# Window attention and vertical convolution on one core: pixels stored by pair of tiles, value products of both column parities at once, whole-tile products in parts

## The chip, the cores and the metric

The kernel runs on one core of a Trainium2 chip. The metric is the device time of one execution in microseconds; before the change it is 3428.8 us, the median of three runs (3424.14 to 3431.46). One more execution was recorded by the hardware profiler; its span is 3428.1 us, and all readings of the profile below are of that execution. The engines are called PE (matrix products; PEld is its weight load), DVE (vector), ACT (scalar), POOL (general) and SP (which issues the transfers here).

## The reference

Everything is float32. The input x is [2, 128, 256, 256]: two images of 128 channels. Two layers follow one another, each as "x = x + layer(groupnorm(x))", with 32 groups of 4 channels.

Layer 0 is a halo attention. A 1x1 projection gives q, k and v (4 heads of 32). Queries come in 8x8 windows, keys and values in 12x12 windows around them. The scores get a relative position term by row and by column, and a fixed mask:

```
table[0::2, :] = -np.inf
table[:, 0::2] = -np.inf
...
attn = jnp.einsum('bnd,bmd->bnm', q, k)
attn = attn + rel_pos_emb(q, rel_height, rel_width) + FIXED_MASK
attn = jax.nn.softmax(attn, axis=-1)
out = jnp.einsum('bnm,bmd->bnd', attn, v)
```

Because of the mask, a query sees only keys of its own row parity and its own column parity. So each window falls apart into four small attentions: for one row parity r and column parity c there are 4x4 = 16 queries and 6x6 = 36 keys. An output projection of 128x128 ends the layer.

Layer 1 is a 5-tap vertical convolution over all channels, a 3-tap depthwise one after it, times a grouped 3-tap horizontal product that is spread over channels.

## The kernel before, in words

**Units.** `attention_fast` walks over strips of 8 image rows (k = 0 to 63, 32 per image), and within each over the two row parities r. A pair (k, r) is a unit, u = 2k + r; there are 128. A strip has 32 windows side by side; two neighbours make a pair, so there are NPAIR = 16 pairs.

**Pixels.** `normalise(k)` turns ten rows of input into `f_xn`, a tile [128 channels, row parity, column parity, 131 columns, 6 rows]: for one parity, one column after the other, six rows each. There are two such tiles, used in turn. DVE does this with two scalings (L282), one per column parity; POOL copies the two rows that the strip shares with the one before (L275). A pair of windows needs 10 columns of one parity, 60 elements; it takes 64 from offset 48 n, and the next pair's begin two columns before these end. Thus the shared columns are stored once, and a pair's 64 elements of one column parity lie together, but those of the other parity lie far away.

**The products of a unit, in PE's order.** The order on every engine is written out by hand (`manual_schedule`).
- `biases` (L399, tile `f_s`): 32 matmul records of 32x64 that add the position terms.
- `scores` (L415, `f_s`): 128 records, 64 rows by 64 columns. ACT then takes the exponent (L424).
- `values` (L380, `f_pv`): the pixels are the stationary side, 64 of them, and the 128x128 value weights stream. One product for each of 16 pairs and 2 column parities, written to partitions 0 to 63 or 64 to 127. ACT copies one half of each bank to `f_vt`, DVE the other (L386).
- `coefficients` (L356, `f_pa`) for the next strip: 16 products of 64 columns with `f_xq`, pixels ordered by place, which POOL copies out of `f_xn` (`by_place`, L293, four copies per unit). ACT and DVE evacuate to `f_cf`.
- `attend` (L440, `f_o`): 128 records of 128 rows by 32 columns.
- `queries` (L333, `f_pq`), `keys` (L312, `f_pk`) of the next unit and `project` (L473, `f_py`) of this one: two products each, full 128x128 weights, 512 columns streamed, each filling one of the four rotating banks `ps_pj`.

A float32 product is one matmul in the program and two weight loads and two matmuls in the trace: 27,431 against 54,862. The products at the start of the kernel (L210) that fold the position tables into the query weights are cut in four per head.

`convolutions_fast` (L561 on) is the second layer. The change doesn't touch it.

Of the kernel before, what the change touches and what calls it, by code (L numbers as in the profile page):

```python
# [9 lines left out]
F32 = mybir.dt.float32  # L10
I32 = mybir.dt.int32
AF = mybir.ActivationFunctionType
ALU = mybir.AluOpType
# [6 lines left out]
P = 128  # L20
W = 256
HEADS = 4
DH = 32
NREL = 23
# [119 lines left out]
def attention_fast(tc, io, x1_d, norm, st_x, st_y, tags, ends):  # L144
# [6 lines left out]
    with ExitStack() as l0:  # L151
# [16 lines left out]
        wkT = wqkvT[:, P : 2 * P]  # L168
        wvT = wqkvT[:, 2 * P : 3 * P]

        xn = [cst.tile([P, 2, 2, XC, 6], F32, tag=f"f_xn{i}", name=f"f_xn{i}") for i in range(2)]
        kt = [
            [cst.tile([P, 2, XC, 6], F32, tag=f"f_kt{r}{i}", name=f"f_kt{r}{i}") for i in range(2)]
            for r in range(2)
# [6 lines left out]
            for g in range(2)  # L181
        ]

        xq = cst.tile([P, 4, 2, 4, 4, NPAIR], F32, tag="f_xq", name="f_xq")
        wb = cst.tile([P, 4, 4, HEADS, 16], F32, tag="f_wb", name="f_wb")
        for i in range(2):
            nc.gpsimd.memset(xn[i], 0.0)
# [7 lines left out]
        with ExitStack() as setup:  # L195
            sp = setup.enter_context(tc.tile_pool(name="f_setup", bufs=6))


            wq_nat = sp.tile([P, P], F32, tag="wq_nat", name="f_wq_nat", bufs=1)
            nc.sync.dma_start(wq_nat, io["w_q"])  # L200
            relT = sp.tile([P, 2 * NREL], F32, tag="relT", name="f_relT", bufs=1)
            nc.sync.dma_start(relT, io["relT"])
            g_rel = sp.tile([P, HEADS, 2 * NREL], F32, tag="g_rel", name="f_g_rel", bufs=1)
            for h in range(HEADS):
                pg = ps_pj.tile([P, 512], F32, tag="pj", name=f"f_pg_{h}")


                for o in (0, NREL):
                    for m in (0, 64):
                        nc.tensor.matmul(  # L210
                            pg[m : m + 64, o : o + NREL], wq_nat[32 * h : 32 * h + 32, m : m + 64],
                            relT[32 * h : 32 * h + 32, o : o + NREL], start=True, stop=True,
                        )
                nc.scalar.mul(g_rel[:, h, :], pg[:, : 2 * NREL], SCALE)
            for t in range(4):
                o = 11 - 2 * t
                for t1 in range(4):
                    nc.scalar.copy(wb[:, t, t1, :, 0:6], g_rel[:, :, o : o + 11 : 2])
                o = NREL + 11 - 2 * t
                for t2 in range(4):  # L220
                    nc.scalar.copy(wb[:, t2, t, :, 6:12], g_rel[:, :, o : o + 11 : 2])
            for s in range(NS):
                t = sp.tile([P, 8, W], F32, tag="sx", name=f"f_sx_0_{s}")
                nc.sync.dma_start(t, x[0, :, 8 * s : 8 * s + 8, :])
                norm.chunk(st_x[0], 4 * s, t)
# [27 lines left out]
        def load_rows(k):  # L253
# [4 lines left out]
            nc.sync.dma_start(t[:, 0:n, :], x[b, :, 8 * s : 8 * s + n, :])  # L258
            raws[k] = t

        def normalise(k):
            b, s = divmod(k, NS)
            if s == 0:
                norms[b] = norm.group(st_x[b], ps_pj, f"x{b}")
                st_y[b] = norm.new(f"st_y{b}", tags[(2 * b + 2) % 3])
                if b + 1 < NB:
                    st_x[b + 1] = norm.new(f"st_x{b + 1}", tags[(2 * b + 1) % 3])
            mean, rstd = norms[b]
            cur, prev = xn[k % 2], xn[(k + 1) % 2]
            cells = cur.rearrange("p r c j i -> p (r c) j i")  # L270
            if s == 0:
                nc.gpsimd.memset(cells[:, :, :, 0:1], 0.0)
                lo = 0
            else:
                nc.gpsimd.tensor_copy(  # L275
                    cells[:, :, :, 0:2], prev.rearrange("p r c j i -> p (r c) j i")[:, :, :, 4:6]
                )
                lo = 1
            hi = min(10, H - 8 * s) // 2
            rows = raws[k].rearrange("p (i r) (j c) -> p c r j i", r=2, c=2)  # L280
            for c in range(2):
                nc.vector.tensor_scalar(  # L282
                    cur[:, :, c, 1:129, 1 + lo : 1 + hi], rows[:, c, :, :, lo:hi], mean, rstd,
                    ALU.subtract, ALU.mult,
                )
            if hi < 5:
                nc.gpsimd.memset(cells[:, :, :, 1 + hi : 6], 0.0)

        def by_place(k, columns):
            cells = xn[k % 2].rearrange("p r c j i -> p (r c) j i")[:, :, 1:129, 1:5]  # L290
            for t2 in columns:
                for half in range(2):
                    nc.gpsimd.tensor_copy(  # L293
                        xq[:, t2, half],
                        cells[:, :, 64 * half : 64 * half + 64].rearrange(
                            "p a (m b) i -> p b i a m", b=4
                        )[:, t2],
                    )

        def old_keys(u):  # L300
            k, r = divmod(u, 2)
            if k % NS > 0:
                nc.gpsimd.tensor_copy(kt[r][k % 2][:, :, :, 0:2], kt[r][(k + 1) % 2][:, :, :, 4:6])

        def keys(u):
            k, r = divmod(u, 2)
            s = k % NS
            cur, xt = kt[r][k % 2], xn[k % 2]

            def part(c):  # L310
                pk = ps_pj.tile([P, 512], F32, tag="pj", name=f"f_pk_{u}_{c}")
                nc.tensor.matmul(pk, wkT, xt[:, r, c, 1:129, 2:6], start=True, stop=True)  # L312
                nc.scalar.copy(cur[:, c, 1:129, 2:6], pk.rearrange("p (j i) -> p j i", i=4))

            def top():

                pk = ps_pj.tile([P, 512], F32, tag="pj", name=f"f_pk_{u}_top")
                nc.tensor.matmul(pk, wkT, xt[:, r, :, 1:129, 0:2], start=True, stop=True)
                nc.scalar.copy(
                    cur[:, :, 1:129, 0:2], pk.rearrange("p (c j i) -> p c j i", c=2, i=2)  # L320
                )

            return ([top] if s == 0 else []) + [lambda c=c: part(c) for c in range(2)]

        def queries(u):

            k, r = divmod(u, 2)
            q = wk.tile([P, 2, NPAIR, 2, 32], F32, tag="q", name=f"f_q_{u}")
            qs[u] = q

            def part(c):
                pq = ps_pj.tile([P, 512], F32, tag="pj", name=f"f_pq_{u}_{c}")
                nc.tensor.matmul(  # L333
                    pq, wq_s, xn[k % 2][:, r, c, 1:129, 1:5], start=True, stop=True
                )
                for i in range(2):
                    nc.scalar.activation(  # L337
                        q[:, c, :, i], pq.rearrange("p (n x) -> p n x", n=NPAIR), AF.Copy,
                        scale=head[:, i : i + 1],
                    )  # L340

            return [lambda c=c: part(c) for c in range(2)]

        def coefficients(k, r):
# [3 lines left out]


            if r == 0:  # L350
                cfs[k] = wk.tile([P, 2, 4, 8, 2, 16], F32, tag="cf", name=f"f_cf_{k}")
            pa = ps_pj.tile([P, 512], F32, tag="pj", name=f"f_pa_{k}_{r}")
            for t in range(8):
                t2, t1 = 2 * r + t // 4, t % 4
                for half in range(2):
                    nc.tensor.matmul(  # L356
                        pa[64 * half : 64 * half + 64, 64 * t : 64 * t + 64],
                        wb[:, t2, t1].rearrange("p h x -> p (h x)"),
                        xq[:, t2, half, t1].rearrange("p a m -> p (a m)"), start=True, stop=True,
                    )  # L360
            src = pa.rearrange("p (t m e) -> p e m t", t=8, e=2)
            for i in range(2):
                dst = cfs[k][:, :, :, :, i, 8 * r : 8 * r + 8].rearrange("p e a n t -> p e (a n) t")
                if i == 0:
                    nc.scalar.activation(
                        dst, src, AF.Identity, bias=keep[:, 1:2], scale=keep[:, 0:1]
# [5 lines left out]

        def values(u, j):
            k, r = divmod(u, 2)
            xt = xn[k % 2].rearrange("p r c j i -> p r c (j i)")
            pv = ps_pj.tile([P, 512], F32, tag="pj", name=f"f_pv_{u}_{j}")
            for n in range(4):
                o = 48 * (4 * j + n)
                for c in range(2):
                    nc.tensor.matmul(  # L380
                        pv[64 * c : 64 * c + 64, P * n : P * n + P], xt[:, r, c, o : o + 64], wvT,
                        start=True, stop=True,
                    )
            for c in range(2):
                rows = slice(64 * c, 64 * c + 64)
                (nc.vector.tensor_copy if c else nc.scalar.copy)(  # L386
# [4 lines left out]
        def biases(u):  # L391

            k, r = divmod(u, 2)
            for e in range(2):
                for half in range(2):
                    for g in range(2):
                        rows = slice(64 * half + 32 * g, 64 * half + 32 * g + 32)
                        for c in range(2):
# [2 lines left out]
                                    "p n i x -> p (n i) x"  # L401
                                ),
                                hot[rows, e],
                                cfs[k][rows, e, 2 * r + c].rearrange("p n i x -> p (n i x)"),
                                start=e == 0, stop=False, skip_group_check=True,
                            )

# [59 lines left out]
        def project(u):  # L467
# [2 lines left out]
            x1s[u] = x1 = x1p.tile([P, 4, W], F32, tag="x1", name=f"f_x1_{u}")  # L470
            for c in range(2):
                py = ps_pj.tile([P, 512], F32, tag="pj", name=f"f_py_{u}_{c}")
                nc.tensor.matmul(py, woT, ots.pop((u, c)), start=True, stop=True)  # L473
                nc.vector.tensor_tensor(  # L474
                    x1[:, :, c:W:2], py.rearrange("p (m t) -> p t m", t=4), raws[k][:, r:8:2, c:W:2],
                    ALU.add,
# [872 lines left out]
```

## Time and profile before

| what | value |
|---|---|
| median of three runs | 3428.8 us |
| attention, from first coefficients to last projection | about 2131 us (112 to 2243) |
| convolutions | about 1162 us (2258 to 3420) |
| PE busy in the attention | 1987.8 us |
| DVE, ACT, POOL busy in the attention | 1461, 1095, 496 us |
| `f_pv` L380: matmul records, busy | 8192, 493.4 us |
| `f_pq`, `f_pk`, `f_py`: records, busy | 512 each; 265.6, 248.0, 240.3 us |
| `f_xn` L282 on DVE, mean of one | 1290 ns |
| `f_xq` L293 on POOL, mean of one | 746 ns |

"Busy" is the time in which at least one instruction of the group is at work, so records that run side by side count once. The mean of one record is its whole latency and is longer than the distance at which such records follow one another; where a rate matters, the distance between starts is used. In the chain of waits each piece of time goes to the instruction that the end of the kernel hung on; "issue" is time in which an engine stood still and the profile shows nothing it waited for.

### The profile page before, as it was taken

The page shows a single profiled execution, that of the slowest core. Times are in us where ns is not written, and L with a number is a line of the kernel's source. Part 1 is how long each engine was busy: PE and PEld are TensorE (multiplying, and loading weights), DVE is VectorE, ACT ScalarE, POOL GpSimd, SP SyncE. Part 2 cuts the span into 40 slices and gives each one's busy share as a digit, 9 for nine tenths or more (in the row PEclk, how much of TensorE's full clock was granted, in tenths as well). Part 3 has the DMA queues.
Part 4 walks back from the last instruction along what each step waited for, and adds up shares of the span by engine and source line. Part 5 has one row for each costly group of instructions (what it writes and reads, how often), then busy time and mean ns, then how long its engine had stood idle before and what let it go on. Part 6 is the DMA issues. An engine that isn't in the chain of part 4 may idle for free.

```text
span 3428.1 us, 120552 instructions
## 1 busy us (share of the span) xinstructions
PE 3150.4 (92%) x54862; PEld 1911.4 (56%) x54862; DVE 2551.8 (74%) x3827; ACT 1498.2 (44%) x2543; POOL 950.2 (28%) x854
## 2 busy tenths in 40 slices
PE   0798999999989899999999999989999999999998
PEld 0566766666666677677676667633333334333333
DVE  8576766767767676666666666668888888888887
ACT  0444544544545455555555555523333333333332
POOL 1212221222222122222222212123333333333333
PEclk9999999999999999999999999999999999999999
DMA  9323322323223221221221222133333332333332
GB/s 396 111 96 111 109 102 87 118 92 113 103 103 113 76 80 65 80 84 66 80 84 66 80 70 81 46 102 114 114 123 123 123 122 96 113 112 123 123 123 83
DMA packets 115912, 360.56 MB, mean 105 GB/s; under 512 B 8001, under 2 KB 74305, under 8 KB 90817
## 3 DMA queue, kind: packets, MB, share of 16 engines
q1 hardware_dynamic: 115392, 352.76, 29.2%
q8 instruction: 434, 7.11, 0.8%
q14 instruction: 86, 0.70, 0.1%
HBM read 218.51 MB, written 134.22 MB: 103 GB/s over the span
## 4 chain that ended last, share of the span: by engine, by line
PE 91%; issue 6%; DVE 1%; POOL 1%; DMA 1%; ACT 0%; SPq 0%; POOLq 0%; DVEq 0%
PE a_p L640 26%; PE f_pv L380 14%; PE f_o L440 8%; PE f_s L415 8%; PE f_pq L333 7%; PE f_pk L312 7%; PE f_py L473 6%; PE g L626 5%; PE f_s L399 4%; PE f_pa L356 4%; PE b L710 2%; DMA f_sx<-in_x 0%; DVE t L699 0%; POOL f_xq L293 0%; POOL f_kt L189 0%
## 5 line engine op out<-in xcount | busy, mean ns | idle before, releaser
L386 DVE COPY f_vt<-f_pv 64x512 f32<-64x512 f32 x512 | 354.4, 694 | 414.1 <-ACT f_vt L386 407.6
L640 PE MATMUL a_p<-xm,w 128*128 128x512 f32 (+1 forms) x1288 | 581.4, 597 | 0.0
L293 POOL COPY f_xq<-f_xn 128x256 f32<-128x256 f32 x512 | 358.0, 746 | 760.3 <-DVE f_xn L282 760.3
L380 PE MATMUL f_pv<-f_wqkvT,f_xn 128*64 128x128 f32 x8192 | 493.4, 275 | 19.1 <-issue 18.3
L337 ACT ACTIVATE f_q<-f_pq,f_head 128x512 f32<-128x512 f32 x512 | 311.2, 689 | 419.1 <-PE f_pq L333 418.9
L380 PEld LDWEIGHTS f_pv<-f_wqkvT,f_xn 128*64 128x64 f32 x8192 | 452.2, 137 | 38.0 <-issue 28.9
L424 ACT ACTIVATE f_p<-f_s 128x512 f32<-128x512 f32 x512 | 265.4, 602 | 401.8 <-PE f_s L415 401.8
L699 DVE SCALAR_TENSOR_TENSOR t<-t,w,t 128x1024 f32<-128x1024 f32 x256 | 420.3, 1642 | 6.8 <-ACT t L692 1.7
L640 PEld LDWEIGHTS a_p<-xm,w 128*128 128x128 f32 x1288 | 238.2, 189 | 331.4 <-issue 331.0
L692 ACT ACTIVATE t<-t,w 128x1024 f32<-128x1024 f32 x128 | 147.3, 1150 | 619.7 <-DVE t L687 619.7
L440 PE MATMUL f_o<-f_vt,f_p 128*32 128x66 f32 x16384 | 290.7, 224 | 96.7 <-issue 93.3
L386 ACT COPY f_vt<-f_pv 64x512 f32<-64x512 f32 x512 | 298.7, 584 | 148.1 <-PE f_pv L380 147.2
L440 PEld LDWEIGHTS f_o<-f_vt,f_p 128*32 128x32 f32 x16384 | 254.6, 111 | 118.5 <-issue 105.9
L727 POOL TENSOR_TENSOR y<-y,raw 128x768 f32<-128x768 f32 x62 | 169.5, 2734 | 541.0 <-DVE y L719 493.0
L275 POOL COPY f_xn<-f_xn 128x1048 f32<-128x1048 f32 x62 | 71.8, 1158 | 890.5 <-PE f_pv L380 890.5
L728 POOL TENSOR_TENSOR y<-y,raw 128x1280 f32<-128x1280 f32 x64 | 246.4, 3849 | 164.3 <-DVE y L719 164.3
L415 PEld LDWEIGHTS f_s<-f_q,f_kt 64*64 64x64 f32 x16384 | 253.4, 135 | 59.0 <-issue 58.6
L415 PE MATMUL f_s<-f_q,f_kt 64*64 64x64 f32 x16384 | 272.6, 220 | 7.7 <-issue 7.7
L333 PE MATMUL f_pq<-f_xn,f_wq_s 128*128 128x512 f32 x512 | 265.6, 641 | 1.3 <-DVE f_on L447 1.3
L474 DVE TENSOR_TENSOR f_x<-f_py,f_raw 128x512 f32<-128x512 f32 x256 | 175.5, 690 | 113.7 <-PE f_py L473 113.6
L312 PE MATMUL f_pk<-f_xn,f_wqkvT 128*128 128x512 f32 x512 | 248.0, 605 | 0.0
L473 PE MATMUL f_py<-f_ot,f_woT 128*128 128x512 f32 x512 | 240.3, 591 | 1.7 <-DVE f_ot L458 1.7
(115 smaller groups left out, 4012.6 us busy)
## 6 DMA issues: line engine op xcount, KB each, us to landing
f_raw<-in_x SPq DMA_DIRECT2D x62, 1280.0 KB, 8.8
f_sx<-in_x SPq DMA_DIRECT2D x64, 1024.0 KB, 7.8
f_x<-f_x SPq DMA_DIRECT2D x128, 512.0 KB, 3.9
out<-y SPq DMA_DIRECT2D x64, 1024.0 KB, 4.9
raw<-f_x SPq DMA_DIRECT2D x64, 640.0 KB, 6.5
raw<-f_x SPq DMA_DIRECT2D x62, 384.0 KB, 7.0
f_raw<-in_x SPq DMA_DIRECT2D x2, 1024.0 KB, 8.0
raw_pre<-f_x SPq DMA_DIRECT2D x2, 384.0 KB, 5.1
```

Of the source, the lines that this page charges most:

```text
L293: nc.gpsimd.tensor_copy(xq[:, t2, half], cells[:, :, 64 * half : 64 * half + 64].rearrange("p a (m b) i -> p b i a m", b=4)[:, t2],)
L312: nc.tensor.matmul(pk, wkT, xt[:, r, c, 1:129, 2:6], start=True, stop=True)
L333: nc.tensor.matmul(pq, wq_s, xn[k % 2][:, r, c, 1:129, 1:5], start=True, stop=True)
L337: nc.scalar.activation(q[:, c, :, i], pq.rearrange("p (n x) -> p n x", n=NPAIR), AF.Copy, scale=head[:, i : i + 1],)
L380: nc.tensor.matmul(pv[64 * c : 64 * c + 64, P * n : P * n + P], xt[:, r, c, o : o + 64], wvT, start=True, stop=True,)
L386: (nc.vector.tensor_copy if c else nc.scalar.copy)(vt[rows, 4 * j : 4 * j + 4, :, c, 0:32], pv[rows].rearrange("p (n h d) -> p n h d", n=4 ...
L415: nc.tensor.matmul(sc[g][n // 8][64 * c : 64 * c + 64, n % 8].rearrange("p i x -> p (i x)"), keys_k[rows, c, 48 * n : 48 * n + 64], qs[u][ ...
L424: nc.scalar.activation(pts[u][:, g, 8 * half : 8 * half + 8].rearrange("p n i x -> p (n i x)"), sc[g][half].rearrange("p n i x -> p (n i x ...
L440: nc.tensor.matmul(po[32 * h : 32 * h + 32, n - lo], p[:, h // 2, n, h % 2], vt[:, n, h], start=True, stop=True,)
L473: nc.tensor.matmul(py, woT, ots.pop((u, c)), start=True, stop=True)
L640: nc.tensor.matmul(pa[:, : n * W], w, rows, start=i == 0, stop=i == len(terms) - 1)
L699: nc.vector.scalar_tensor_tensor(t3[:, j : j + 4], t1[:, j + tap : j + tap + 4, :], w3[:, tap : tap + 1], t3[:, j : j + 4], ALU.mult, ALU.add,
```

## The change

The pixels are stored by pair of windows: `f_xn` becomes [128, row parity, 16 pairs, 2 column parities, 64], each cell 10 columns of 6 rows and 4 unused elements. Columns that two neighbouring pairs share are stored in both. Now a pair's pixels of both column parities are 128 elements in a row, and one product with 128 stationary columns gives the values of both; its rows land on partitions 0 to 63 and 64 to 127 as before.

It brings: four scalings instead of two in `normalise`, and two new DVE copies that fill the shared columns; other access patterns for the products that read pixels, and for POOL's copies; key rows of the strip before copied by column parity (two POOL copies for one). Queries, keys and projection no longer go as one product of 512 columns, but in 3, 2 and 2 parts. The setup products at L210 are no longer cut. The order of `f_xq` and `f_cf` follows the new order of pixels.

```
-        xn = [cst.tile([P, 2, 2, XC, 6], F32, tag=f"f_xn{i}", name=f"f_xn{i}") for i in range(2)]
+        xn = [cst.tile([P, 2, NPAIR, 2, 64], F32, tag=f"f_xn{i}", name=f"f_xn{i}") for i in range(2)]
...
-                for o in (0, NREL):
-                    for m in (0, 64):
-                        nc.tensor.matmul(
-                            pg[m : m + 64, o : o + NREL], wq_nat[32 * h : 32 * h + 32, m : m + 64],
-                            relT[32 * h : 32 * h + 32, o : o + NREL], start=True, stop=True,
-                        )
+                nc.tensor.matmul(
+                    pg[:, : 2 * NREL], wq_nat[32 * h : 32 * h + 32, :],
+                    relT[32 * h : 32 * h + 32, :], start=True, stop=True,
+                )
...
+            for r in range(2):
+                for c in range(2):
+                    nc.vector.tensor_scalar(
+                        inner(k, r, c, 1 + lo, 1 + hi), rows[:, r, c, :, :, lo:hi], mean, rstd,
+                        ALU.subtract, ALU.mult,
+                    )
+            new = slice(1 + lo, 1 + hi)
+            nc.vector.tensor_copy(cells[:, :, 2:32, 0, new], cells[:, :, 0:30, 8, new])
+            nc.vector.tensor_copy(cells[:, :, 0:30, 9, new], cells[:, :, 2:32, 1, new])
...
                     nc.gpsimd.tensor_copy(
-                        xq[:, t2, half],
-                        cells[:, :, 64 * half : 64 * half + 64].rearrange(
-                            "p a (m b) i -> p b i a m", b=4
-                        )[:, t2],
+                        xq[:, t2, half].rearrange("p t r n c e -> p r t (n c) e"),
+                        cells[:, :, 16 * half : 16 * half + 16, 1 + t2 : 9 : 4, 1:5].rearrange(
+                            "p r a e i -> p r i a e"
+                        ),
                     )
...
+        def in_parts(count, dst, w, moving):
...
+            cuts = [NPAIR * i // count for i in range(count + 1)]
+            for lo, hi in zip(cuts, cuts[1:]):
+                nc.tensor.matmul(dst[:, 32 * lo : 32 * hi], w, moving[:, lo:hi], start=True, stop=True)
...
-                nc.tensor.matmul(pk, wkT, xt[:, r, c, 1:129, 2:6], start=True, stop=True)
+                in_parts(2, pk, wkT, inner(k, r, c, 2, 6))
...
-                nc.tensor.matmul(
-                    pq, wq_s, xn[k % 2][:, r, c, 1:129, 1:5], start=True, stop=True
-                )
+                in_parts(3, pq, wq_s, inner(k, r, c, 1, 5))
...
-                o = 48 * (4 * j + n)
-                for c in range(2):
-                    nc.tensor.matmul(
-                        pv[64 * c : 64 * c + 64, P * n : P * n + P], xt[:, r, c, o : o + 64], wvT,
-                        start=True, stop=True,
-                    )
+                nc.tensor.matmul(
+                    pv[:, P * n : P * n + P], xn[k % 2][:, r, 4 * j + n].rearrange("p c x -> p (c x)"),
+                    wvT, start=True, stop=True,
+                )
...
-                nc.tensor.matmul(py, woT, ots.pop((u, c)), start=True, stop=True)
+                in_parts(2, py, woT, ots.pop((u, c)).rearrange("p (n x) -> p n x", n=NPAIR))
```

More of the change, by code (lines that the diff above doesn't have):

```diff
@@ L182, in attention_fast @@
         ]
-        xq = cst.tile([P, 4, 2, 4, 4, NPAIR], F32, tag="f_xq", name="f_xq")
+        xq = cst.tile([P, 4, 2, 4, 2, 8, 2, 2], F32, tag="f_xq", name="f_xq")
         wb = cst.tile([P, 4, 4, HEADS, 16], F32, tag="f_wb", name="f_wb")
@@ L259, in load_rows, with by_cell, inner @@
             raws[k] = t
+        def by_cell(k):
+            return xn[k % 2][..., 0:60].rearrange("p r n c (j i) -> p r (n c) j i", i=6)
+        def inner(k, r, c, lo, hi):
+            return by_cell(k)[:, r, c::2, 1:9, lo:hi]
         def normalise(k):
@@ L268, in normalise @@
             mean, rstd = norms[b]
-            cur, prev = xn[k % 2], xn[(k + 1) % 2]
-            cells = cur.rearrange("p r c j i -> p (r c) j i")
+            cells = by_cell(k)
+            flat = cells.rearrange("p r a j i -> p (r a) j i")
             if s == 0:
-                nc.gpsimd.memset(cells[:, :, :, 0:1], 0.0)
+                nc.gpsimd.memset(flat[:, :, :, 0:1], 0.0)
                 lo = 0
@@ L275, in normalise @@
                 nc.gpsimd.tensor_copy(
-                    cells[:, :, :, 0:2], prev.rearrange("p r c j i -> p (r c) j i")[:, :, :, 4:6]
+                    flat[:, :, :, 0:2],
+                    by_cell(k + 1).rearrange("p r a j i -> p (r a) j i")[:, :, :, 4:6],
                 )
@@ L279, in normalise @@
             hi = min(10, H - 8 * s) // 2
-            rows = raws[k].rearrange("p (i r) (j c) -> p c r j i", r=2, c=2)
-            for c in range(2):
-                nc.vector.tensor_scalar(
-                    cur[:, :, c, 1:129, 1 + lo : 1 + hi], rows[:, c, :, :, lo:hi], mean, rstd,
-                    ALU.subtract, ALU.mult,
-                )
+            rows = raws[k].rearrange("p (i r) (n j c) -> p r c n j i", r=2, n=NPAIR, c=2)
+            for r in range(2):
[7 more added lines that the diff above has]
+            nc.vector.tensor_copy(cells[:, :, 0:30, 9, new], cells[:, :, 2:32, 1, new])
             if hi < 5:
-                nc.gpsimd.memset(cells[:, :, :, 1 + hi : 6], 0.0)
+                nc.gpsimd.memset(flat[:, :, :, 1 + hi : 6], 0.0)
         def by_place(k, columns):
-            cells = xn[k % 2].rearrange("p r c j i -> p (r c) j i")[:, :, 1:129, 1:5]
+            cells = by_cell(k)
             for t2 in columns:
@@ L302, in old_keys @@
             if k % NS > 0:
-                nc.gpsimd.tensor_copy(kt[r][k % 2][:, :, :, 0:2], kt[r][(k + 1) % 2][:, :, :, 4:6])
+                for c in range(2):
+                    nc.gpsimd.tensor_copy(kt[r][k % 2][:, c, :, 0:2], kt[r][(k + 1) % 2][:, c, :, 4:6])
+        def in_parts(count, dst, w, moving):
+            cuts = [NPAIR * i // count for i in range(count + 1)]
+            for lo, hi in zip(cuts, cuts[1:]):
+                nc.tensor.matmul(dst[:, 32 * lo : 32 * hi], w, moving[:, lo:hi], start=True, stop=True)
         def keys(u):
@@ L307, in keys @@
             s = k % NS
-            cur, xt = kt[r][k % 2], xn[k % 2]
+            cur = kt[r][k % 2]
             def part(c):
                 pk = ps_pj.tile([P, 512], F32, tag="pj", name=f"f_pk_{u}_{c}")
-                nc.tensor.matmul(pk, wkT, xt[:, r, c, 1:129, 2:6], start=True, stop=True)
+                in_parts(2, pk, wkT, inner(k, r, c, 2, 6))
                 nc.scalar.copy(cur[:, c, 1:129, 2:6], pk.rearrange("p (j i) -> p j i", i=4))
@@ L317, in top @@
                 pk = ps_pj.tile([P, 512], F32, tag="pj", name=f"f_pk_{u}_top")
-                nc.tensor.matmul(pk, wkT, xt[:, r, :, 1:129, 0:2], start=True, stop=True)
+                for c in range(2):
+                    nc.tensor.matmul(
+                        pk[:, W * c : W * c + W], wkT, inner(k, r, c, 0, 2), start=True, stop=True
+                    )
                 nc.scalar.copy(
@@ L350, in coefficients @@
             if r == 0:
-                cfs[k] = wk.tile([P, 2, 4, 8, 2, 16], F32, tag="cf", name=f"f_cf_{k}")
+                cfs[k] = wk.tile([P, 2, 2, 8, 2, 2, 16], F32, tag="cf", name=f"f_cf_{k}")
             pa = ps_pj.tile([P, 512], F32, tag="pj", name=f"f_pa_{k}_{r}")
@@ L358, in coefficients @@
                         wb[:, t2, t1].rearrange("p h x -> p (h x)"),
-                        xq[:, t2, half, t1].rearrange("p a m -> p (a m)"), start=True, stop=True,
+                        xq[:, t2, half, t1].rearrange("p r n c e -> p (r n c e)"), start=True, stop=True,
                     )
@@ L362, in coefficients @@
             for i in range(2):
-                dst = cfs[k][:, :, :, :, i, 8 * r : 8 * r + 8].rearrange("p e a n t -> p e (a n) t")
+                dst = cfs[k][..., i, 8 * r : 8 * r + 8].rearrange("p e r n c t -> p e (r n c) t")
                 if i == 0:
@@ L374, in values @@
             k, r = divmod(u, 2)
-            xt = xn[k % 2].rearrange("p r c j i -> p r c (j i)")
             pv = ps_pj.tile([P, 512], F32, tag="pj", name=f"f_pv_{u}_{j}")
             for n in range(4):
-                o = 48 * (4 * j + n)
-                for c in range(2):
-                    nc.tensor.matmul(
-                        pv[64 * c : 64 * c + 64, P * n : P * n + P], xt[:, r, c, o : o + 64], wvT,
-                        start=True, stop=True,
-                    )
+                nc.tensor.matmul(
+                    pv[:, P * n : P * n + P], xn[k % 2][:, r, 4 * j + n].rearrange("p c x -> p (c x)"),
+                    wvT, start=True, stop=True,
+                )
             for c in range(2):
@@ L403, in biases @@
                                 hot[rows, e],
-                                cfs[k][rows, e, 2 * r + c].rearrange("p n i x -> p (n i x)"),
+                                cfs[k][rows, e, r, :, c].rearrange("p n i x -> p n (i x)"),
                                 start=e == 0, stop=False, skip_group_check=True,
```

## The prediction

> **What bounds the kernel now.** I read the page's busy line and chain first, then the chain in time, then PE's waits, then the DMA queues.
>
> ```profile
> PE 3150.4 (92%) x54862; PEld 1911.4 (56%) x54862; DVE 2551.8 (74%) x3827; ACT 1498.2 (44%) x2543; POOL 950.2 (28%) x854
> PE 91%; issue 6%; DVE 1%; POOL 1%; DMA 1%; ACT 0%; SPq 0%; POOLq 0%; DVEq 0%
> ```
>
> PE sets the end nearly everywhere. But 6% (206 us) of its chain is "issue": PE waits for nothing the profile knows. One such piece of 86.5 us is the start; the rest lies in the attention. Two stretches of the chain in time show how (start, length, what):
>
> ```profile
> 1005.45 2.22 PE f_pv L380 x37
> 1007.66 0.89 issue
> 1008.55 1.64 PE f_pv L380 x26
> 1010.19 0.06 PE f_pa L356
> 1010.24 0.05 PE f_pv L380
> 1010.30 0.93 PE f_pa L356 x30
> 1011.23 1.16 PE f_o L440 x69
> 1012.39 1.88 issue
> 1014.26 1.11 PE f_o L440 x59
> 1015.38 1.92 PE f_pq L333 x4
> ```
>
> ```profile
> 363.95 0.93 PE f_pa L356 x32
> 364.88 1.98 PE f_o L440 x128
> 366.86 1.92 PE f_pq L333 x4
> 368.77 1.75 PE f_pk L312 x4
> 370.53 1.72 PE f_py L473 x4
> ```
>
> In the first, two holes; in the second, the same work without any. Count the matmuls between the holes: 27 f_pv, 31 or 32 f_pa and 69 f_o make 128, each with its weight load: 256 instructions. Numbering all of PE's instructions in the trace, I find that nearly every hole stands at a number that leaves 193 or 194 when divided by 256. The queue for instructions has the same size in it:
>
> ```profile
> q8 instruction: 434, 7.11, 0.8%
> ```
>
> 7.11 MB in 434 packets is 16,384 bytes each, and PE's 110,771 instructions over 434 are 255. So PE runs dry at the seam between two blocks of instructions. Excess over each pair of lines' usual distance between matmul starts, within 10 instructions of such a seam, sums to 163 us over the attention. (The next list has less, as it counts a hole only from a modelled matmul end.)
>
> ```profile
> PE f_o L440 <- issue: 93.3, 80, 3.3
> PE f_pv L380 <- issue: 18.3, 39, 1.4
> PE f_pa L356 <- POOL f_xq L293: 6.0, 5, 5.2
> ```
>
> Other engines hardly hold PE: POOL's 6.0 us is among the largest. A unit (half a strip; 128 of them) without holes takes 15.0 us between query starts; the mean is 2131/128 = 16.6. After a long hole the granted clock is 0.5 for 3.4 to 6.8 us (query products then 853 ns apart instead of 430); away from seams that costs about 20 us more.
>
> **What the skill says.** (1) "Runtime: NRT & Kernel Launch", Instruction fetch mechanics: instructions arrive in blocks of 16 KiB, 256 of them, the next fetched while the current runs, the cost "mostly hidden". The size agrees; the hiding doesn't: 163 us. (2) "TensorEngine Tiling (Array Packing)", Key Properties: changing the tiling mode drains PE. Agrees: from the last f_py to the first f_s is 522 ns against 428 within f_py, so 94. (3) "TensorE: Matmul & The Clock Gate", LDWEIGHTS: the load takes columns/1.2 ns. Agrees: loads of 32, 64 and 128 columns last 111, 137 and 189 ns, 0.81 ns per column, so 128 columns stream in about 105. (4) "GPSIMD Engine Reference", Performance pitfalls for Q7 kernels: reading at a step over 8 bytes costs half as much again per element. Agrees in direction: f_xq (step 24 elements) 746 ns for 256, f_xn L275 (pairs) 1158 for 1048.
>
> **Part by part, per unit.**
>
> *Values.* 32 products of 64 columns become 16 of 128. Each f32 product leaves two loads and two matmuls in the trace, so 64 pairs of instructions become 32. PE time isn't halved: the column halves already run together, starts 7 ns apart, one pair per 109 ns: 32 x 109 = 3.49 us. The new ones stream the same 128 elements, and their loads (105) are just as long. Low bound 109 ns. High bound, a load not hidden at all: 107 + 105 = 212, 6.8 us. Nearest row: the 64x64 scores also have load equal to stream (53 ns) and come every 58, 5 over the stream. And the 128-column loads of f_py hide behind their 428 ns. I take 112: 3.58, +0.1 us.
>
> *Mode.* Scores to values drained already; the first load is now 64 columns longer, +0.05. Values to coefficients (128x64) kept the mode and now switch: 94 + 53 for the first load, +0.15.
>
> *Parts.* Keys 2 to 4 products, queries 2 to 6, projection 2 to 4: 8 more products, 16 more pairs. A part of 160 columns or more streams longer than its load, so only the fixed part of a matmul is paid: 429 ns for 512 columns against 427 at the slope of 128 columns in 107. 16 x 2 to 5 = 0.03 to 0.08; I take 0.05.
>
> Sum: +0.35 us, x128 = +45 us (range 30 to 65, without the bad load).
>
> *Instructions.* 799 PE instructions per unit (waits included) in the built program become 768 = 3 x 256. The seam moves 31 places per unit before; afterwards it stays put. The smaller setup products (L210: 16 to 4) only shift its place. With the seam at the same number as in the trace, and what comes ahead of the program unchanged, I find it in units 2 to 61 at places 236 (inside scores), 492 (41 instructions into f_o) and 748 (between keys and projection); in units 66 to 126 at 214, 470 (19 into f_o) and 726 (second query product).
>
> The trace of before has every place sampled, so the cost can be read off. Seams from the biases to two thirds of the scores: no hole. First 50 instructions of f_o: 0.2 us in the mean (1.2 in one of five or so). Between keys and projection, or just into the latter: none in seven. In the second query product: one 1.5 among four. For contrast, late scores to early values 0.3 to 0.8, and the last third of f_o to the first query product 1.0 to 1.6. It is the length of a block that decides: blocks of 2 to 4 us of work wait 0.7 to 1.0, of 4 to 5.5 us 0.3 to 0.5, longer ones hardly. The new blocks have about 4.4, 5.8, 5.5 us, later 6.2, 5.7, 3.9. I take 0.15 per unit in the first half and 0.43 in the second: 60 x 0.15 + 62 x 0.43 = 36 us. Gain 163 - 36 = 127. With fewer long holes the half clock shrinks, 20 to 6: 14 more.
>
> *DVE and POOL.* Per strip the normalisation becomes four scalings of 512 elements for two of 1024 (1290 ns each; I take 4 x 0.63, about equal) and two copies of 240, about 0.35 us each by the 128x320 f_on at 491: +0.8 us. POOL's f_xq waits for that, then four copies, then the coefficients. In an undisturbed unit POOL's fourth copy ended 0.54 us ahead of f_pa. But f_pa now starts 0.3 later and needs copies 3 and 4 only half-way (0.5 us on): slack is about 0.5. f_xq's pattern gains a dimension, inner run 2 instead of 16, the step unchanged: between 746 ns and, as a high bound, 1.1 us. At 746 nothing waits; I take +5 us in all. The halo copy L275 (1280 for 1048 elements) and the split key copies lie on POOL, idle 72%; DVE has 3 us free per unit. The longer start adds 1.
>
> **Sum:** 3428.8 - 127 - 14 + 45 + 5 + 1 = 3339.
>
> **Rivals.**
> (B) A wait on POOL takes the holes' place: copies at 1.1 us put the fourth 1.4 later, about 1 us over the slack in 64 strips: +64, 3400. For it: POOL is on the path, and the new pattern isn't in the trace. Against: pairs are no slower there, and the matmuls wait copy by copy.
> (C) The seam falls elsewhere, and then in every unit. 48 places later it would stand 249 into f_o, 1.6 us, with 0.2 elsewhere: 1.8 x 128 = 230 against 163, +67, and PE's +45: 3428.8 + 112 = 3540, slower. For it: the place is inferred. Against: the code ahead of the first changed product is the same.
> (D) The 128-column loads aren't hidden: 32 x 105 ns x 128 = +430 us, about 3765, slower. Against: f_py's loads.
>
> **How the numbers follow.** Forecast 0.67, B 0.17, C 0.09, D 0.04; the rest (0.03) for a gain eaten by small costs near no change. The forecast's parts run from 30 to 65 for PE and 15 to 70 for left seams: 3295 to 3385; with B the range is 3292 to 3408. Faster 0.86, same 0.02, slower 0.12.
>
> **What would show it.** PE's "issue" waits in f_o should fall from 93 us to under 30 and stand in one or two places of the unit; f_pv busy should stay near 3.6 us per unit; the gap from f_pv to f_pa be near 250 ns; PE waits for f_xq under 20 us. A large f_pa wait for POOL means B; holes in every unit C; f_pv at 200 ns a record D.

## The result and the profile after

The changed kernel takes 3297.65 us (median of 4 runs, 3295.96 to 3302.73), beside 3428.39 us before (median of 4 runs; the 3428.8 above was of three): ratio 0.9622, 95% interval 0.9605 to 0.9639, 131 us less. The prediction had 3339 us and a range of 3292 to 3408, so the time lies 41 us under the forecast and 6 us above the range's lower end.

The page after, first the busy line, then the chain by engine:

```profile
PE 3143.8 (95%) x52798; PEld 2244.1 (68%) x52798; DVE 2628.0 (80%) x4083; ACT 1499.9 (46%) x2543; POOL 935.7 (28%) x978
PE 95%; issue 2%; DVE 1%; POOL 1%; DMA 1%; ACT 0%; SPq 0%; POOLq 0%; DVEq 0%
```

PE is busy for 3143.8 us against 3150.4: it hardly changes. (Busy time is not work here: time at half clock counts as busy, and of that the attention has less.) What is gone is waiting: "issue" falls from 6% to 2% of the chain. Three of PE's waits after (what waited, for whom: us, times, longest):

```profile
PE pm_x L119 <- issue: 85.5, 1, 85.5
PE f_pa L378 <- DVE f_vt L405: 9.9, 2, 5.1
PE f_pa L378 <- POOL f_xq L306: 5.9, 2, 5.7
```

The first is the start, which was 86.5 before. The 93.3 us of `f_o` and 18.3 of `f_pv` are no longer in the list of waits at all, and POOL's 6.0 stayed at 5.9. One unit in the chain in time:

```profile
1000.49 2.08 PE f_pq L324 x12
1002.57 1.75 PE f_pk L324 x8
1004.33 1.73 PE f_py L324 x8
1006.05 1.05 PE f_s L418 x32
1007.10 2.02 PE f_s L434 x128
1009.13 3.77 PE f_pv L399 x32
1012.89 1.08 PE f_pa L378 x32
1013.98 1.98 PE f_o L459 x128
1015.95 2.08 PE f_pq L324 x12
```

From query products to query products there is no hole: 15.46 us. Without holes the kernel before took 15.01, so the work on PE became 0.46 us per unit *longer*. The accounts over the attention: a unit took 16.68 us in the mean before, 1.67 over its undisturbed time, and takes 15.67 after, 0.20 over. There are 127 distances between the starts of 128 units: 212 us of loss became 25, a gain of 187, and the longer unit costs 58. The difference, 129, is nearly all of the 131.

### The profile page after: what moved, and what is told of

Its sections match the earlier page's. It is cut to its first block, busy times and chain, and to the rows that moved or that the text cites. A ratio compares the mean times of both kernels' runs of the same rounds, so it can differ in the third digit from the quotient of the medians.

```text
span 3294.9 us, 117110 instructions
## 1 busy us (share of the span) xinstructions
PE 3143.8 (95%) x52798; PEld 2244.1 (68%) x52798; DVE 2628.0 (80%) x4083; ACT 1499.9 (46%) x2543; POOL 935.7 (28%) x978
## 4 chain that ended last, share of the span: by engine, by line
PE 95%; issue 2%; DVE 1%; POOL 1%; DMA 1%; ACT 0%; SPq 0%; POOLq 0%; DVEq 0%
PE a_p L659 27%; PE f_pv L399 14%; PE f_pq L324 8%; PE f_s L434 8%; PE f_o L459 8%; PE f_pk L324 7%; PE f_py L324 7%; PE g L645 5%; PE f_pa L378 4%; PE f_s L418 4%; PE b L729 2%; DMA f_sx<-in_x 0%; DVE t L718 0%; POOL f_xn L189 0%; DMA raw<-f_x 0%
## 5 line engine op out<-in xcount | busy, mean ns | idle before, releaser
L306 POOL COPY f_xq<-f_xn 128x256 f32<-128x256 f32 x512 | 309.1, 648 | 763.7 <-DVE f_xn L292 763.7
L399 PE MATMUL f_pv<-f_wqkvT,f_xn 128*128 128x128 f32 x4096 | 491.3, 278 | 0.0
L399 PEld LDWEIGHTS f_pv<-f_wqkvT,f_xn 128*128 128x128 f32 x4096 | 466.9, 192 | 8.6
L283 POOL COPY f_xn<-f_xn 128x1280 f32<-128x1280 f32 x62 | 86.7, 1398 | 780.7 <-PE f_pv L399 780.7
L324 PE MATMUL f_pq<-f_xn,f_wq_s 128*128 128x160 f32 (+1 forms) x1536 | 277.0, 327 | 0.9 <-issue 0.9
L459 PE MATMUL f_o<-f_vt,f_p 128*32 128x66 f32 x16384 | 264.6, 223 | 0.0
L459 PEld LDWEIGHTS f_o<-f_vt,f_p 128*32 128x32 f32 x16384 | 243.2, 111 | 9.1
L324 PE MATMUL f_py<-f_ot,f_woT 128*128 128x256 f32 x1024 | 243.2, 380 | 2.3 <-DVE f_ot L477 2.3
L324 PE MATMUL f_pk<-f_xn,f_wqkvT 128*128 128x256 f32 x1024 | 245.3, 380 | 0.0
L324 PEld LDWEIGHTS f_pq<-f_xn,f_wq_s 128*128 128x128 f32 x1536 | 234.7, 188 | 13.9 <-issue 1.5
```

The lines of the kernel that those rows point to most:

```text
L306: nc.gpsimd.tensor_copy(xq[:, t2, half].rearrange("p t r n c e -> p r t (n c) e"), cells[:, :, 16 * half : 16 * half + 16, 1 + t2 : 9 : 4, ...
L324: nc.tensor.matmul(dst[:, 32 * lo : 32 * hi], w, moving[:, lo:hi], start=True, stop=True)
L399: nc.tensor.matmul(pv[:, P * n : P * n + P], xn[k % 2][:, r, 4 * j + n].rearrange("p c x -> p (c x)"), wvT, start=True, stop=True,)
L459: nc.tensor.matmul(po[32 * h : 32 * h + 32, n - lo], p[:, h // 2, n, h % 2], vt[:, n, h], start=True, stop=True,)
```

## The experiments

Each ratio is to the kernel before, run on the same chip. "Holes" are excess over the usual distance of matmul starts at the seams of 256 instructions, counted as in the prediction, and put down to the product that they follow: 163 us before, 1.7 after. An "undisturbed" unit is one without holes or waits. A "place" is an instruction's number within its unit, counted from the biases.

**The seam's place alone.** The setup products are cut in four again, nothing else:

```
+                for o in (0, NREL):
+                    for m in (0, 64):
+                        nc.tensor.matmul(
+                            pg[m : m + 64, o : o + NREL], wq_nat[32 * h : 32 * h + 32, m : m + 64],
...
-                nc.tensor.matmul(
-                    pg[:, : 2 * NREL], wq_nat[32 * h : 32 * h + 32, :],
```

> The changed kernel with one thing undone: the setup products at the start are cut in four per head as before, 48 more PE instructions ahead of the loop, nothing else. Theory (the gain is where the seams between blocks of 256 PE instructions stand): they move 48 places, one of them to some 226 to 248 instructions into f_o, which in the kernel before cost 1.1 to 1.6 us; about 195 us of holes in all, time near 3500 us (3430 to 3560). Rival (the gain is that PE has fewer instructions or cheaper value products): no change, 3298 us.

Measured 3448.77 us, 1.0052 (1.0034 to 1.0069): twelve small products more at the start, 48 instructions, more than undo the gain. The ends of two units in its chain in time:

```profile
999.15 2.44 issue
1001.59 0.31 PE f_o L461 x5
1001.90 2.72 PE f_pq L326 x12
...
1017.00 1.96 PE f_o L461 x123
1018.95 0.44 issue
1019.39 0.31 PE f_o L461 x5
1019.71 2.08 PE f_pq L326 x12
```

Each hole stands with 5 matmuls of `f_o` left. In 59 units of the first image the hole is at exactly this place, in 51 units of the second with 16 left: the seams stay put, and all 129 us of holes are in `f_o`. In the first unit shown the queries take 2.72 us instead of 2.08, for the clock is granted at a half from 1003.1 us on, for 3.4 us. The theory's 195 us of holes were too many (129); the rival, no change, is out.

**The parts undone.**

```
-                in_parts(3, pq, wq_s, inner(k, r, c, 1, 5))
+                in_parts(1, pq, wq_s, inner(k, r, c, 1, 5))
```

and likewise 1 for keys and projection.

> The changed kernel with queries, keys and projection as whole products of 512 columns again: 736 PE instructions per unit in place of 768. Theory: the seams move 32 places per unit, so all places are met and about 2.9 seams per unit cost the 0.4 us of before each, 150 us of holes; whole products themselves save up to 0.15 us per unit; time near 3440 us (3400 to 3470). Rival (the joined value products bring the gain, the parts are a cost or neutral): 3298 us or less, near 3280.

Measured 3389.04 us, 0.9876 (0.9854 to 0.9897); holes 92 us. Holes come back, fewer than the 150 us expected, and the time lies under the expected range; the run on storage without joined values bears on this. An undisturbed unit takes 15.42 us, so the parts cost PE only 0.05 per unit.

**Only the setup of the change, in the kernel before.**

> The kernel before with only the setup products of the change (one per head). Theory: its seams move 31 places per unit anyway, so a shift of 48 instructions changes which unit meets which place and not how often; 3428 us within 10. Rival (the smaller setup is worth something by itself): faster by more than that.

```
-                for o in (0, NREL):
-                    for m in (0, 64):
...
+                nc.tensor.matmul(
+                    pg[:, : 2 * NREL], wq_nat[32 * h : 32 * h + 32, :],
```

Measured 3419.96 us, 0.997 (0.9957 to 0.9982). With seams that move 31 places per unit the same edit is worth 9 us, not 150; holes are 158 us.

**Storage without joined values.** The pixels of the change, but one value product per column parity, and whole products:

```
+                for c in range(2):
+                    nc.tensor.matmul(
+                        pv[64 * c : 64 * c + 64, P * n : P * n + P], xn[k % 2][:, r, 4 * j + n, c],
+                        wvT, start=True, stop=True,
+                    )
```

> The changed kernel's storage of pixels with the value products of the kernel before (one per column parity, 64 columns) and whole products for queries, keys and projection: 800 PE instructions per unit. Theory (the storage itself gives nothing, the seams drift as before): the holes of before, 163 us, come back, and queries cost 0.1 us more per unit for the storage; 3445 us (3425 to 3465). Rival (the storage by pair is itself a gain): under 3400 us.

Measured 3452.58 us, 1.0092 (1.0072 to 1.0111), holes 171 us. So the storage by itself gains nothing: its undisturbed unit is 0.14 us longer than before. Joining the values then takes it to 0.9876, although an undisturbed unit grows from 15.15 to 15.42 us: holes in `f_pv` fall from 30 to 2 us and in `f_o` from 115 to 66, in keeping with a block of 256 instructions that now holds more work. Bringing the unit to 768 does the rest, 92 to 1.7.

**768 by other means.** Whole products, and eight extra ones of one column whose results nobody reads:

```
+                if lo == 0:
+                    for i in range(8):
+                        h = i % 4
+                        nc.tensor.matmul(
+                            bank[32 * h : 32 * h + 32, 500 + i // 4 : 501 + i // 4],
+                            p[:, h // 2, 0, h % 2], vt[:, 0, h, 0, 0:1], start=True, stop=True,
+                        )
```

> The changed kernel with whole products, 736 instructions per unit, and 8 extra products of one column at the head of attend, into a part of the bank that nobody reads: again 768 instructions per unit; the seams stand at 4, 260 and 516 in units 2 to 61 and at 238, 494 and 750 from unit 66 on. Theory (768 and the places count, not the parts): no holes, PE 0.1 us per unit longer than in the changed kernel, 3311 us (3295 to 3330), against 3389 for the same whole products without the extra ones. Rival (the parts themselves help, by giving the fetch more time): 3389 us or more.

Measured 3306.0 us, 0.9663 (0.9646 to 0.9681). More work, and 83 us less than without it. Its chain in time, with the extra products as L460:

```profile
1002.48 1.08 PE f_pa L378 x32
1003.56 0.23 PE f_o L460 x16
1003.79 1.87 PE f_o L466 x128
1005.66 2.07 PE f_pq L324 x4
```

Holes are 2.2 us. The parts as such are not the cause. One block here, from place 4 to 260, holds only about 2.5 us of work and still no hole follows it, so the length of a block alone doesn't decide. The packets of the instruction queue show what happens: in 58 units the packet that follows on this block starts 1.0 us (median) *before* PE reaches place 4, and lands 2.4 us before PE reaches the next seam. Why it starts so early here isn't shown.

**Other parts.** Queries whole, keys and projection in three parts, again 768:

```
-                in_parts(3, pq, wq_s, inner(k, r, c, 1, 5))
+                in_parts(1, pq, wq_s, inner(k, r, c, 1, 5))
...
-                in_parts(2, pk, wkT, inner(k, r, c, 2, 6))
+                in_parts(3, pk, wkT, inner(k, r, c, 2, 6))
...
-                in_parts(2, py, woT, ots.pop((u, c)).rearrange("p (n x) -> p n x", n=NPAIR))
+                in_parts(3, py, woT, ots.pop((u, c)).rearrange("p (n x) -> p n x", n=NPAIR))
```

> The changed kernel with the queries whole and keys and projection in three parts each: again 768 PE instructions per unit, the seams 8 places later. Theory: no holes, as in the changed kernel; the query products lose the 0.17 us per unit by which the parts in the changed kernel are longer than the whole products of before, keys and projection gain at most 0.05; 3298 minus 15, 3283 us (3275 to 3300). Rival (the longer queries come from the new layout of the pixels and not from the parts): 3298 us or a little more.

Measured 3299.18 us, 0.9613 (0.9598 to 0.9628). The time fits the rival, and so does the trace: whole query products come every 468 ns here, 430 in the kernel before. So it is the storage that slows the queries, and hardly the parts.

**The storage moved by one and by three elements.**

```
+        xn_all = [cst.tile([P, 4096 + 8], F32, tag=f"f_xn{i}", name=f"f_xn{i}") for i in range(2)]
+        xn = [
+            t[:, 1 : 1 + 4096].rearrange("p (r n c x) -> p r n c x", r=2, n=NPAIR, c=2) for t in xn_all
+        ]
```

> The changed kernel with the tile of pixels moved by one element (4 bytes); nothing else, PE's instructions are the same. In the changed kernel a query part of 5 or 6 pairs takes 147 or 177 ns, 12 to 15 over its stream, while key parts lie 4 over it; queries start 28 bytes into a cell, keys 32. Theory (queries pay for where their runs lie in memory): with queries at 32 bytes the 12 parts of a unit lose some 0.15 us, 128 units 19 us; 3279 us (3272 to 3288). Rival (each step from pair to pair costs PE the same wherever the runs lie): 3298 us.

> As the shift by one, with three elements (12 bytes): queries start at 40 bytes of a cell, keys at 44. Theory (the place in memory decides, by pieces of 32 bytes that a pair's run touches: 7 for queries now, 6 for keys): queries become as fast as with a shift by one, keys, with 7 pieces, as slow as queries are now, 8 parts of 8 pairs at 2 ns each, plus 0.13 us per unit; about 3295 us (3285 to 3302). Rival (no effect of the place): 3298 us.

Measured 3281.17 us, 0.9591 (0.9577 to 0.9606), and 3296.84, 0.9639 (0.9621 to 0.9658). Lines of the groups (mean ns after the busy time); the changed kernel, then shift one, then shift three:

```profile
L324 PE MATMUL f_pq<-f_xn,f_wq_s 128*128 128x160 f32 x1024 | 207.0, 321 | 0.9 <-issue 0.9
L324 PE MATMUL f_pk<-f_xn,f_wqkvT 128*128 128x256 f32 x1024 | 245.3, 380 | 0.0
```

```profile
L327 PE MATMUL f_pk<-f_xn,f_wqkvT 128*128 128x256 f32 x1024 | 241.5, 377 | 0.0
L327 PE MATMUL f_pq<-f_xn,f_wq_s 128*128 128x160 f32 x1024 | 197.0, 313 | 0.1
```

```profile
L327 PE MATMUL f_pk<-f_xn,f_wqkvT 128*128 128x256 f32 x1024 | 259.4, 394 | 0.0
L327 PE MATMUL f_pq<-f_xn,f_wq_s 128*128 128x160 f32 x1024 | 196.3, 312 | 0.0
```

By distance of starts, query parts of 5 and 6 pairs go from 147 and 177 ns to 138 and 165 with either shift; key parts of 8 pairs from 220 to 216 with one element, and to 233 with three. The count of 32-byte pieces that a pair's run touches (queries 7, 6, 6; keys 6, 6, 7 for no shift, one, three) gives the three large steps; it doesn't explain keys' 4 ns with no shift, and as a rule it rests on these three placements alone. The shift by one has a price off the critical path: POOL's copy of the shared rows into `f_xn` goes from 1398 to 2050 ns.

The shift by one beats both kernels, so it was run again beside the changed kernel on one chip:

> The changed kernel as it is, once more, beside the shift by one element on the same chip: 3298 us (3293 to 3303). Both theories expect this; it is the base for the next run.

> The shift of the pixels by one element, beside the changed kernel on the same chip. Theory (queries' runs of pixels by place in memory): 16 to 18 us under the changed kernel, 3281 us (3277 to 3285). Rival (the difference between the two calls was one of chips): within 4 us of the changed kernel.

Measured 3296.65 (0.9623, 0.9604 to 0.9642) and 3280.59 us (0.9583, 0.9563 to 0.9604): 16 us less, as expected.

**Less traffic, in the kernel before.** 32 loads of 1 MB are left out; the statistics of the second image are taken of rows of the first.

```
-                nc.sync.dma_start(t, x[b, :, 8 * s : 8 * s + 8, :])
...
-            norm.chunk(st_x[b], 4 * s, sxs.pop(u))
+            norm.chunk(st_x[b], 4 * s, raws[u // 2][:, 0:8, :])
```

> The kernel before without the 32 loads of 1 MB that bring the second image for its statistics while the first image is in the attention; the statistics are taken of the strip that is there already (so the second image is normalised with the first one's numbers; engine work is the same). In the kernel before, all 19 holes over 2 us and 97 of the 163 us of holes lie in the first image's units, and a unit takes 17.2 us there against 16.2. Theory (the holes are the arrival of a block of instructions, and the block queues behind data): no holes over 2 us are left, the first image's holes fall to about the 65 us of the second's, its half clock with them; 3429 minus 40, 3389 us (3365 to 3405). Rival (the holes depend on the place of the seam alone): 3425 us.

Measured 3364.33 us, 0.9822 (0.9805 to 0.9839), 25 us below the expectation and just under its range. No hole over 2 us is left (19 before); the first image's holes fall from 97 to 60 us, the second's stay (66 and 65). The holes get shorter and hardly fewer: over 0.4 us there are about 140 before and 131 here. Half clock in the attention falls from 51 to 7 us. Stretches of the two images, the kernel before first, then this one (length, busy time by engine, granted clock, DMA share, GB/s):

```profile
130.00:1170.00 1040.00, 953.69 (x24114) 695.97 (x24107) 732.34 (x1311) 519.33 (x912) 239.03 (x332) 0.98 0.29 103
1190.00:2200.00 1010.00, 962.90 (x24692) 703.04 (x24684) 681.96 (x1223) 532.90 (x938) 246.03 (x343) 1.00 0.22 74
```

```profile
130.00:1130.00 1000.00, 950.65 (x24525) 697.18 (x24518) 749.34 (x1343) 527.59 (x929) 245.37 (x341) 1.00 0.23 76
1150.00:2150.00 1000.00, 952.33 (x24546) 696.51 (x24533) 675.35 (x1209) 528.13 (x931) 245.04 (x341) 1.00 0.22 75
```

At 76 GB/s instead of 103 PE is busy for 95% of the first image's stretch (950.65 of 1000 us), as in the second's; before, it was 92% (953.69 of 1040). Lighter traffic isn't how the changed kernel lost its holes, though: from 130 to 1090 us it moves 112 GB/s, where the kernel before moves 104.

The trace also ties the holes to packets. Of 139 holes over 0.4 us in the kernel before, 9 in 10 end 1.23 to 1.57 us after a packet of the instruction queue has landed (96 holes of the run with the setup cut: 1.25 to 1.52). In the median a packet starts 1.3 us after PE passes the seam before (4.1 or more in one of twenty, ahead of the seam in others), and takes 1.0 us. That makes some 3.7 us from seam to readiness, while a block inside `f_o` is used up in 2. In the changed kernel, from unit 2 on, every packet of the attention lands at least 1.2 us before PE reaches its seam.

## Why the prediction was right, step by step

- *The cause.* PE running dry at seams of 256 instructions: shown, by the moved seam (3298 to 3449), by 768 with extra products (3389 to 3306), by the packets' landing, and by the shorter holes under less traffic.
- *768 and its places.* Right: without the setup edit the other 151 us are not there. Rival C named this very place, 249 instructions into `f_o` (48 instructions more ahead of the loop put the seams 48 places earlier in the unit, not later as it says); it came to 129 us of holes where the prediction had 230, and to 3449 where it had 3540. Its mechanism was right and its place's cost overstated.
- *Left holes, 36 us.* This is the term most off: 1.7 were left, and half clock in the attention fell from 51 to 17 us. With 187 us gained against 141 it outweighed the other miss, PE's longer unit, and the sum came out 41 us too high. What failed is the reading that a block's length decides. Blocks of 4 to 5.5 us had holes of 0.3 to 0.5 us before; the changed kernel has 124 of that length in the first image, and no hole. In the second image 63 of its blocks hold 3.1 to 4.0 us, and no hole of 0.4 us or more follows them. Most of these blocks open at the seam in `f_o`, and there the packet starts 0.4 us after the seam (median); over all seams of the kernel before it was 1.3. So the packet's start counts as much as the block's length, and the samples of before, few at each place (one of 1.5 us among four made 0.3), carried over badly. What sets the start stays open.
- *Values.* 112 ns per record was predicted, and the distance between starts is 112 for all after the first. Two things gave it: the load time of columns/1.2 ns in the Trainium skill ("TensorE: Matmul & The Clock Gate", LDWEIGHTS), which the traces bear out (`f_pv` loads last 137 ns with 64 columns and 192 with 128, 55 more; estimated from the page it is 53), and the nearest row, `f_s`. At 112 ns a load of about 105 hides behind a stream of 107. Rival D is out. `f_pv` and `f_pa` together grew from 4.58 to 4.85 us per unit, 0.28, where the prediction had 0.30 for values and mode.
- *Parts, +0.05 us.* The count was right for the parts (15.47 against 15.42). But the queries' new storage was costed at nothing. From first query to first key start a unit took 1.824 us before and takes 1.993 after, 0.17 more or 21 us in all, and 1.978 with whole products, so 0.15 of it is the storage. That is why PE's +45 became +58; the shift by one element wins 16 us back.
- *DVE and POOL, +5 us.* No wait: POOL's fourth copy ends 0.68 us ahead of `f_pa` (median), 0.63 before. Rival B fell, in part for reasons that nobody had given. DVE takes longer than assumed: the four scalings are busy for 2.85 us per strip where the two were for 2.49, and the two shared-column copies take 297 and 739 ns where 350 each was assumed. But POOL waits for the scalings only and starts beside the first shared-column copy. And its copies are faster, 648 ns against 746, below the range of 746 to 1100 that the prediction gave them. That these two about cancel the later scalings was luck.

## What to carry to other kernels

When the chain shows "issue" on an engine that should never wait, number that engine's instructions and see whether the holes lie at a fixed distance. If a loop's body is near a whole number of blocks, filling it up to that number, even with dead work, keeps the seams in place, and then a few instructions ahead of the loop decide where. Try several places: here a block almost wholly of short `f_o` products cost 129 us, and others cost next to nothing. Such a gain belongs to the whole program: an edit elsewhere that changes the count can lose it, as 48 instructions did here, so look at where the seams stand before two variants are compared.

## What the runs showed of the hardware

- Instruction blocks compete with data: in the kernel before, at 103 GB/s, there are 19 holes over 2 us, and with its traffic cut to 76 GB/s none.
- A long hole can be paid twice: in the kernel before the clock is granted at a half 11 times in the attention, for 3.4 or 6.8 us (query products 853 ns apart), and 8 of these begin within 2 us of the end of a hole of 2.7 us or more.
- Reading pixels for a matmul depends on where the runs lie: moved by 4 bytes, 165 ns instead of 177 for 192 columns; moved by 12 bytes instead of 4, 233 instead of 216 for 256.
- A DVE copy of 240 elements takes 297 ns; the next one of the same size takes 739 (medians of 60 strips). POOL's copies of `f_xq` start during the first. That POOL is the cause was not tried.
